# A two-layer adaLN block: a half-size first and last chunk, modulations as weighted sums, grouped low-rank merges, and an opening in written order

## Chip, core and metric

The kernel runs on one core of a Trainium2 chip. The metric is the device time of one execution in microseconds (us); lower is better. All arithmetic is fp32.

## The reference, cut to what matters

Input x is [2048, 512]: 2048 tokens of 512 channels. Two layers follow, each with six modulation rows of 512 from a condition vector c (`wmod` is [512, 3072]):

```python
mod = (silu(c) @ wmod).reshape(1, 6, 1, 512); sa, ca, ga, sb, cb, gb = mod.swapaxes(0, 1)
ga = sign(ga) * max(|ga|, 0.25); gb = sign(gb) * max(|gb|, 0.25)

# layer 0: block-masked linear, then a gated MLP of 1376 hidden units, every weight with a rank-16 update
x = x + ga * (( layernorm(x) * (1 + ca) + sa) @ (weight * blockmask).T + bias)
h = layernorm(x) * (1 + cb) + sb
x = x + gb * lora(silu(lora(h, gate)) * lora(h, up), down)      # lora(x, w) = x @ w.T + (x @ a.T) @ b.T

# layer 1 (its own c and wmod): a Mamba mixer of 1024 channels and 16 states, then top-2 of 8 rank-16 experts
xz = (layernorm(x) * (1 + ca) + sa) @ W_in.T;  u = silu(causal_conv4(xz[:, :1024]))
ts, B, C = rms(u @ W_x.T split 32, 16, 16);    dt = softplus(ts @ W_dt.T + b_dt)
state = state * exp(dt * A) + (dt * u) * B     # per channel and state, a scan over the 2048 tokens
y = sum over states(state * C) + u * D
x = x + ga * ((y * silu(xz[:, 1024:])) @ W_out.T)
h = layernorm(x) * (1 + cb) + sb
x = x + gb * (h @ base_W.T + 2 * sum over the top 2 experts(rw * (h @ A_e) @ B_e))
```

## The kernel before

Tokens are cut into eight chunks of 256 (`TC`, `NC`, `NM` = 2 token tiles of 128). Channels lie on partitions; the eight channel tiles of the scan (`ND`) lie side by side in one free dimension, so that one scan instruction of 128x2064 takes a whole chunk for one state (8 x (256 + 2 padding)).

**Opening.** Everything is scheduled by the framework's planner, engine by engine, from its cost model. `mod_col` makes a modulation column with 16 small matmuls over four loaded weight tiles (L118), `mod_gate` a gate row with four wide matmuls on a spread condition vector (L126 to L142). The attention weight is masked (L199 to L208) and scaled by the gate. `wide_tile` (L231) loads a gate or up tile, makes its low-rank product with four matmuls of 16 rows (L241), adds it on DVE (L245) and stores the merged tile to DRAM scratch; `down_tile` (L249) does this for the down projection after a scaling on POOL. Chunks after the first read the merged tiles back. `first_layer(0)` runs to its end, then layer one's columns are made, then `front(0)`: norm, input projection (L371), convolution (L391), the small projection, `steps` (softplus, L427), `inputs` and the first `decays`.

**Norm.** `norm_t` (L144): stats on DVE, two POOL instructions for the inverse deviation (L151, L152), the subtraction and scaling on DVE (L156), transposes on PE (L164) and modulation on ACT (L167).

**Main loop** (L654 to L702). For each chunk and each of 16 states: hb = dt*u*B (L669) and the scan (L671) on DVE, hc = h*C (L677) on DVE, PE transposes that add hc into four PSUM banks `ys` (L441), and `decays` for the next state on ACT (L458). `da`, `hb` and `hc` have two buffers each. Between the states, two generators are advanced by budgets: `first` (layer 0 of the next chunks) by 3.6 per state, 8.0 for the first eight states of chunk 0; `second` (`beside(c)`: out_proj and experts of the chunk before, gate_proj of this one, `front` of the next) by 4.8, or 2.5. `late_setup` (the second layer's remaining modulations and the scaled W_out, written to scratch) runs beside chunk 0, its loads on ACT's queue. Streamed weights are loaded on SP's queue into twelve `ws` buffers; `rows_bc` broadcasts B and C three states ahead, on SP as well.

**Tail.** After the last state the last chunk's gating, out_proj and experts run alone.

Of the kernel before, what the change touches and what calls it, by code (L numbers as in the profile page):

```python
# [9 lines left out]
FP = mybir.dt.float32  # L10
# [7 lines left out]
P = 128  # L18
L, DM = 2048, 512
TC = 256  # L20
NC, NM, NK = L // TC, TC // P, DM // P
# [5 lines left out]
SEG = TC + 2  # L27
# [10 lines left out]
def mamba_block_kernel(  # L38
# [36 lines left out]
    def halves(t):  # L75
        return t.rearrange("p (a n) -> p a n", a=2)
# [9 lines left out]
    ones = keep.tile([1, P], FP, name="ones")  # L86
# [4 lines left out]
    def load(c):  # L91
        xs[c] = []
        for i in range(c * NM, (c + 1) * NM):
            xt = xpool.tile([P, DM], FP, tag="x", name="x")
            nc.sync.dma_start(out=xt, in_=x_in[i * P : (i + 1) * P, :])
            xs[c].append(xt)

    da = [keep.tile([P, ND, SEG], FP, name=f"da{i}") for i in range(2)]
    hb = [keep.tile([P, ND, SEG], FP, name=f"hb{i}") for i in range(2)]
    hc = [keep.tile([P, ND, TC], FP, name=f"hc{i}") for i in range(2)]  # L100
    dtu = keep.tile([P, ND, TC], FP, name="dtu")
    dt = keep.tile([P, ND, TC], FP, name="dt")
    states = keep.tile([P, NS, ND], FP, name="states")

    def mod_weights(wmod, j, queue):
        wms = []
        for k in range(NK):
            wm = ws()
            queue.dma_start(out=wm, in_=wmod[k * P : (k + 1) * P, j * DM : (j + 1) * DM])
            wms.append(wm)  # L110
        return wms

    def mod_col(name, sc, wmod, j, queue):
        wms = mod_weights(wmod, j, queue)
        ps = bank()
        for f in range(NK):
            for k in range(NK):
                T.matmul(  # L118
                    ps[:, f : f + 1], lhsT=wms[k][:, f * P : (f + 1) * P], rhs=sc[:, k : k + 1],
                    start=k == 0, stop=k == NK - 1,  # L120
                )
        col = keep.tile([P, NK], FP, name=f"mod_{name}{j}")
        V.tensor_scalar(col, ps[:, :NK], 1.0 if j in (1, 4) else 0.0, None, ALU.add)
        return col

    def spread(sc):  # L126
        scb = tmp()
        scb3 = scb.rearrange("p (k m) -> p k m", k=NK)
        V.tensor_copy(scb3, sc.unsqueeze(2).to_broadcast([P, NK, P]))
        return scb3  # L130

    def mod_gate(scb3, wmod, j, queue):
        wms = mod_weights(wmod, j, queue)
        ps = bank()
        for k in range(NK):
            T.matmul(ps, lhsT=scb3[:, k, :], rhs=wms[k], start=k == 0, stop=k == NK - 1)
# [7 lines left out]
    def norm_t(xt, scale, shift, tag):  # L144
        st = small.tile([P, NM, 6], FP, tag="st", name="st")
        mv = small.tile([P, NM, 2], FP, tag="mv", name="mv")
        for m in range(NM):
            V.bn_stats(st[:, m, :], xt[m])
            V.bn_aggr(mv[:, m, :], st[:, m, :])  # L149
        rs = small.tile([P, NM], FP, tag="rs", name="rs")  # L150
        G.tensor_scalar(rs, mv[:, :, 1], LN_EPS, None, ALU.add)  # L151
        G.tensor_tensor(rs, rs, power, ALU.pow)  # L152
        xn = []
        for m in range(NM):
            t = tmp()
            V.tensor_scalar(t, xt[m], mv[:, m, 0:1], rs[:, m : m + 1], ALU.subtract, ALU.mult)  # L156
            xn.append(t)
        h = hpool.tile([P, NK, TC], FP, tag=tag, bufs=2 if tag == "h0" else 1, name="h")
        for k2 in range(NK // 2):
            ps = halves(bank())  # L160
            for i in range(2):
                k = 2 * k2 + i
                for m in range(NM):
# [6 lines left out]
            yield 0.5  # L170
# [6 lines left out]

    load(0)
    S.activation(c0_sb, c0_sb, AF.Silu)
    w_attn = [ws() for k in range(NK)]  # L180
    for k in range(NK):
        nc.scalar.dma_start(out=w_attn[k], in_=w_attn_t[k * P : (k + 1) * P, :])
# [3 lines left out]
    for k in range(NK):  # L186
        mk = wsp.tile([P, DM], I32, tag="w", name="mk")
        nc.scalar.dma_start(out=mk, in_=mask_t[k * P : (k + 1) * P, :])
# [3 lines left out]

    sa, ca = (mod_col("a", c0_sb, wmod0, j, nc.sync) for j in (0, 1))
    scb0 = spread(c0_sb)
    ga = mod_gate(scb0, wmod0, 2, nc.sync)

# [7 lines left out]
    V.tensor_scalar(on, ps[:, :nb], 0.0, None, ALU.is_gt)  # L204
    for k in range(NK):
# [3 lines left out]
    attn_s = dram.tile([NK, P, DM], FP, name="attn_s")  # L209
    for k in range(NK):  # L210
        V.tensor_tensor(w_attn[k], w_attn[k], ga, ALU.mult)
        nc.gpsimd.dma_start(out=attn_s[k], in_=w_attn[k])
    V.tensor_tensor(bias_row, bias_row, ga[0:1, :], ALU.mult)

    sb, cb = (mod_col("a", c0_sb, wmod0, j, nc.scalar) for j in (3, 4))
    gb = mod_gate(scb0, wmod0, 5, nc.scalar)

    ranks = [hc[0].rearrange("p t n -> p (t n)")[:R, i * DM : (i + 1) * DM] for i in range(3)]
    wides = [t.rearrange("p t n -> p (t n)")[:R, :FF] for t in (da[0], da[1], hb[0])]
    for dst, src in zip(ranks + wides, (gate_a, up_a, down_bt, gate_bt, up_bt, down_a)):  # L220
        nc.gpsimd.dma_start(out=dst, in_=src)
    ga_r, ua_r, db_r = ranks
    gb_w, ub_w, da_w = wides
    V.tensor_tensor(db_r, db_r, gb[:R, :], ALU.mult)

    gate_s = dram.tile([len(HT), P, DM], FP, name="gate_s")
    up_s = dram.tile([len(HT), P, DM], FP, name="up_s")
    down_s = dram.tile([len(HT), P, DM], FP, name="down_s")
    wout_s = dram.tile([ND, P, DM], FP, name="wout_s")

    def wide_tile(src, scratch, a_r, b_w, j, first):  # L231
        h0, n = HT[j]
        w = ws()
        w3 = w[:, : NK * n].rearrange("p (k n) -> p k n", k=NK)
        if not first:
            nc.sync.dma_start(out=w[:, : NK * n], in_=scratch[j][:, : NK * n])
            return w3
        nc.sync.dma_start(out=w3, in_=src.rearrange("(k p) n -> p k n", p=P)[:, :, h0 : h0 + n])
        ps = bank()
        for k in range(NK):  # L240
            T.matmul(  # L241
                ps[:, k * n : (k + 1) * n], lhsT=a_r[:, k * P : (k + 1) * P], rhs=b_w[:, h0 : h0 + n],
                start=True, stop=True,
            )
        V.tensor_tensor(w[:, : NK * n], w[:, : NK * n], ps[:, : NK * n], ALU.add)  # L245
        nc.gpsimd.dma_start(out=scratch[j][:, : NK * n], in_=w[:, : NK * n])
        return w3

    def down_tile(j, first):  # L249
        h0, n = HT[j]  # L250
        w = ws()
        if not first:
            nc.sync.dma_start(out=w[:n, :], in_=down_s[j][:n, :])
            return w
        nc.sync.dma_start(out=w[:n, :], in_=down_t[h0 : h0 + n, :])
        G.tensor_tensor(w[:n, :], w[:n, :], gb[:n, :], ALU.mult)
        ps = bank()
        T.matmul(ps[:n, :], lhsT=da_w[:, h0 : h0 + n], rhs=db_r, start=True, stop=True)
        V.tensor_tensor(w[:n, :], w[:n, :], ps[:n, :], ALU.add)
        nc.gpsimd.dma_start(out=down_s[j][:n, :], in_=w[:n, :])  # L260
        return w

    done = set()

    def first_layer(c):
        xt = xs[c]
# [515 lines left out]
```

## Time and profile before

| | |
|---|---|
| three runs | median 1860.17 us (1859.12 to 1862.04) |
| the profiled execution | 1859.38 us, span 1857.6 us |
| first scan starts | 246.9 us |
| 128 scans of 128x2064 | 4.45 us each |
| hb and hc, 128x2048 | 2.28 us each |
| decays on ACT, 128x256, 1024 of them | 0.50 us each |
| busy over the span | PE 84%, DVE 80%, ACT 51%, POOL 12% |

PE is the matmul engine (its weight loads are listed apart, as PEld), DVE the vector engine, ACT the scalar engine, POOL the GpSimd engine, SP the engine that only issues DMAs. Every fp32 matmul appears as two matmul records. Lines are those of the kernel before.

### The profile page before, as it was taken

What the parts mean: (1) busy time and instruction counts of PE and PEld (TensorE: products, weight loads), DVE (VectorE), ACT (ScalarE), POOL (GpSimd) and SP (SyncE); (2) the same over time, 40 slices, a digit from 0 to 9 for tenths busy, and PEclk for the clock granted to TensorE, in tenths of its full rate; (3) what the DMA queues carried; (4) which work ended last, traced back from release to release, by engine and by line L of the source; (5) the groups of instructions that cost most, each with busy time, mean ns of one, the idle gap of its engine ahead of it and who ended that gap; (6) DMA issues with size and microseconds to landing.
All of it is one profiled execution on the core that took longest, in us unless ns stands there. A gap on an engine that the chain in (4) does not pass through costs nothing. (4 is left out here: it accounts for less than half of the span.)

```text
span 1857.6 us, 18733 instructions
## 1 busy us (share of the span) xinstructions
PE 1562.9 (84%) x6568; PEld 1079.8 (58%) x6568; DVE 1483.0 (80%) x1215; ACT 938.9 (51%) x2005; POOL 225.7 (12%) x211
## 2 busy tenths in 40 slices
PE   4899879988698888999799888999899789768646
PEld 4685647756465665576456665576557565544433
DVE  2222387797978989897999789897989799999992
ACT  0110367445654565565565566466556555674521
POOL 0123010013000200031003300160003000300000
PEclk9689779988998989999899999999999999879768
DMA  8544333562343234432343334422333235213100
GB/s 251 154 154 165 116 86 115 166 198 85 91 126 108 86 93 120 129 102 89 91 137 106 94 100 123 116 83 89 116 115 100 80 104 149 67 35 100 28 20 12
DMA packets 157536, 199.73 MB, mean 108 GB/s; under 512 B 14962, under 2 KB 93682, under 8 KB 157443
## 3 DMA queue, kind: packets, MB, share of 16 engines
q1 hardware_dynamic: 141984, 166.57, 31.0%
q10 hardware_dynamic: 10434, 15.81, 2.6%
q0 software_dynamic: 5024, 16.16, 2.4%
q8 instruction: 52, 0.85, 0.2%
q14 instruction: 42, 0.34, 0.1%
HBM read 182.43 MB, written 16.06 MB: 107 GB/s over the span
## 5 line engine op out<-in xcount | busy, mean ns | idle before, releaser
L671 DVE TENSOR_TENSOR_SCAN hb<-da,hb 128x2064 f32<-128x2064 f32 x128 | 568.7, 4449 | 3.5
L458 ACT ACTIVATE da<-dt,neg_a 128x256 f32<-128x256 f32 x1024 | 430.4, 497 | 55.9 <-DVE hb L671 43.1
L298 PE MATMUL ps<-h,ws 128*128 128x256 f32 (+1 forms) x1408 | 352.6, 407 | 19.6 <-ACT z L481 13.0
L441 PE MATMUL y<-ident,hc 128*128 128x128 f32 x2048 | 287.0, 293 | 65.5 <-DVE hc L677 65.3
L298 PEld LDWEIGHTS ps<-h,ws 128*128 128x128 f32 (+1 forms) x1408 | 281.6, 204 | 93.2 <-issue 19.6
L441 PEld LDWEIGHTS y<-ident,hc 128*128 128x128 f32 x2048 | 255.1, 152 | 117.8 <-DVE hc L677 75.4
L677 DVE TENSOR_TENSOR hc<-hb,bcn 128x2048 f32<-128x2048 f32 x128 | 291.4, 2278 | 35.8 <-PE y L441 35.6
L669 DVE TENSOR_TENSOR hb<-dtu,bcn 128x2048 f32<-128x2048 f32 x128 | 290.7, 2281 | 2.7
L673 ACT COPY states<-hb 128x8 f32<-128x8 f32 x112 | 22.8, 203 | 348.0 <-DVE hb L671 340.1
L151 POOL TENSOR_SCALAR rs<-mv 128x2 f32<-128x2 f32 x32 | 41.3, 1292 | 1155.4 <-DVE mv L149 1139.5
L508 PE MATMUL ps<-ws,tmp 128*128 128x512 f32 x256 | 136.3, 671 | 47.3 <-ACT tmp L502 47.1
L317 PE MATMUL ps<-ws,hidden 128*128 128x512 f32 (+1 forms) x352 | 159.0, 601 | 5.7 <-ACT z L481 4.9
L371 PE MATMUL ps<-h,ws 128*128 128x256 f32 x512 | 122.2, 394 | 2.5 <-ACT h L167 2.5
L476 PE MATMUL ps<-ws,h 128*128 128x512 f32 x256 | 117.1, 604 | 1.1 <-ACT hidden L306 0.6
L317 PEld LDWEIGHTS ps<-ws,hidden 128*128 128x128 f32 (+1 forms) x352 | 65.7, 192 | 85.1 <-issue 71.7
L371 PEld LDWEIGHTS ps<-h,ws 128*128 128x128 f32 x512 | 100.3, 199 | 21.3 <-ACT h L167 5.8
L508 PEld LDWEIGHTS ps<-ws,tmp 128*128 128x128 f32 x256 | 51.2, 214 | 101.3 <-ACT tmp L502 53.5
L309 DVE TENSOR_TENSOR hidden<-hidden,tmp 128x512 f32<-128x512 f32 x40 | 27.6, 690 | 85.1 <-ACT tmp L307 85.1
L391 DVE SCALAR_TENSOR_TENSOR tmp<-xp,ch,tmp 128x256 f32<-128x256 f32 x192 | 79.7, 476 | 13.1 <-ACT tmp L386 12.6
L458 ACT ACT_TABLE_LOAD x67 | 86.0, 1283 | 1.0
L164 PE MATMUL ps<-ident,tmp 128*128 128x128 f32 x256 | 48.7, 329 | 41.4 <-DVE tmp L156 38.0
L379 POOL COPY xp<-halo 128x6 f32<-128x6 f32 x28 | 71.0, 2537 | 77.2 <-DVE tmp L391 66.7
(137 smaller groups left out, 1575.0 us busy)
## 6 DMA issues: line engine op xcount, KB each, us to landing
bcn<-bc SPq DMA_DIRECT2D x128, 256.0 KB, 5.1
ws<-gate_s SPq DMA_DIRECT2D x70, 256.0 KB, 2.7
ws<-up_s SPq DMA_DIRECT2D x70, 256.0 KB, 2.7
ws<-down_s SPq DMA_DIRECT2D x70, 256.0 KB, 3.8
ws<-win_x_t_dram SPq DMA_DIRECT2D x64, 256.0 KB, 3.8
ws<-win_z_t_dram SPq DMA_DIRECT2D x64, 256.0 KB, 2.9
ws<-wout_s SPq DMA_DIRECT2D x64, 256.0 KB, 2.6
ws<-wmod_dram ACTq DMA_DIRECT2D x36, 256.0 KB, 3.2
```

The lines of the kernel that those rows point to most:

```text
L298: T.matmul(ps[:n, i, :], lhsT=w3[:, k, :], rhs=h[:, k, :], stop=k == NK - 1, **start_only(4 * i + k),)
L317: T.matmul(acc[m], lhsT=hidden[j // 2][:n, j % 2, m * P : (m + 1) * P], rhs=w[:n, :], start=j == 0, stop=j == len(HT) - 1,)
L371: T.matmul(ps[:, i, :], lhsT=w3[:, k, :], rhs=h[:, k, :], stop=k == NK - 1, **start_only(4 * i + k),)
L379: G.tensor_copy(xp[:, :, : KC - 1], halo[:, 2 * t2 : 2 * t2 + 2, :])
L391: V.scalar_tensor_tensor(acc[:, i, :], xp[:, i, j : j + TC], ch[:, t, C_W + j : C_W + j + 1], acc[:, i, :], ALU.mult, ALU.add,)
L441: T.matmul(ys[m][a][:, i * P : (i + 1) * P], lhsT=src[:, m * P : (m + 1) * P], rhs=ident, start=first and i == 0, stop=last, is_transpose= ...
L458: S.activation(d[:, t, 2:], dt[:, t, :], AF.Exp, scale=neg_a[:, t, n : n + 1])
L476: T.matmul(acc[m], lhsT=h[:, k, m * P : (m + 1) * P], rhs=w, start=k == 0, stop=k == NK - 1)
L508: T.matmul(acc[m], lhsT=g[:, i, m * P : (m + 1) * P], rhs=w, start=t == 0, stop=t == ND - 1)
L669: V.tensor_tensor(h[:, :, 2:], dtu, bcn[:, 0:1, :].to_broadcast([P, ND, TC]), ALU.mult)
L671: V.tensor_tensor_scan(flat_h, flat_d, flat_h, 0.0, ALU.mult, ALU.add)
L677: V.tensor_tensor(hcn, h[:, :, 2:], bcn[:, 1:2, :].to_broadcast([P, ND, TC]), ALU.mult)
```

## The change

The chunks become one of 128 tokens, seven of 256 and one of 128, with the buffers viewed at the chunk's width. A modulation row becomes a weighted sum of four weight tiles (one pass on ACT, three on DVE), summed over partitions by matmuls with ones. The low-rank rows are copied to partitions 0, 32, 64 and 96, and the merges of four tiles are made together with one matmul from each row group into the four banks of `ys`. The norm's subtraction moves to ACT, with two more POOL instructions for its bias. PE and DVE keep the written order until the first decays. `late_setup` moves from chunk 0 to chunk 1, its modulation loads and those of W_out from ACT's queue to SP's; the budgets are given anew.

```diff
-NC, NM, NK = L // TC, TC // P, DM // P
+SIZES = [1, 2, 2, 2, 2, 2, 2, 2, 1]
...
+    def mod_row(sc, wmod, j, wm=None):
...
+        acc = tmp()
+        S.activation(acc, wm[0], AF.Identity, scale=sc[:, 0:1])
+        for k in range(1, NK):
+            V.scalar_tensor_tensor(acc, wm[k], sc[:, k : k + 1], acc, ALU.mult, ALU.add)
+        return acc
     def mod_col(...):
-        for f in range(NK):
-            for k in range(NK):
-                T.matmul(ps[:, f : f + 1], lhsT=wms[k][:, f * P : (f + 1) * P], rhs=sc[:, k : k + 1], ...)
+        acc = mod_row(sc, wmod, j, wm)
+        for f in range(NK):
+            T.matmul(ps[:, f : f + 1], lhsT=acc[:, f * P : (f + 1) * P], rhs=ones[:, 0:1], start=True, stop=True)
     def mod_gate(...):
-        for k in range(NK):
-            T.matmul(ps, lhsT=scb3[:, k, :], rhs=wms[k], start=k == 0, stop=k == NK - 1)
+        acc = mod_row(sc, wmod, j, wm)
+        T.matmul(ps, lhsT=ones, rhs=acc, start=True, stop=True)
...
     def norm_t(xt, scale, shift, tag):
-        G.tensor_scalar(rs, mv[:, :, 1], LN_EPS, None, ALU.add)
-        G.tensor_tensor(rs, rs, power, ALU.pow)
+        G.tensor_scalar(rs[:, 0, :], mv[:, :, 1], LN_EPS, None, ALU.add)
+        G.tensor_tensor(rs[:, 0, :], rs[:, 0, :], power[:, :nm], ALU.pow)
+        G.tensor_tensor(rs[:, 1, :], mv[:, :, 0], rs[:, 0, :], ALU.mult)
+        G.tensor_scalar(rs[:, 1, :], rs[:, 1, :], -1.0, None, ALU.mult)
-            V.tensor_scalar(t, xt[m], mv[:, m, 0:1], rs[:, m : m + 1], ALU.subtract, ALU.mult)
+            S.activation(t, xt[m], AF.Identity, bias=rs[:, 1, m : m + 1], scale=rs[:, 0, m : m + 1])
...
+    def merge_wide(tiles, scratch, a_r, b_w, js):
+        h0, n = HT[js[0]][0], sum(HT[j][1] for j in js)
+        for k in range(NK):
+            r = slice(32 * k, 32 * k + R)
+            T.matmul(y_all[:, k, :n], lhsT=a_r[r, k * P : (k + 1) * P], rhs=b_w[r, h0 : h0 + n], start=True, stop=True)
+        for w3, j in zip(tiles, js):
+            V.tensor_tensor(w3, w3, y_all[:, :, o : o + m], ALU.add)
+            nc.gpsimd.dma_start(out=scratch[j]..., in_=w3)
+    def merge_down(tiles, js):              # the same by groups of four down tiles
...
+        ahead = {                           # in first_layer(0): before the product of hidden tiles j0, j0 + 1
+            0: lambda: merge_next(0, 1),
+            2: lambda: merge_next(1, 1),
+            4: lambda: merge_next(0, 2),
+            6: lambda: (merge_next(1, 2), second_gate()),
+            8: lambda: merge_down_next(0),
+        }
...
+                if j == 6:                  # in first_layer(0), down projection
+                    mods1.extend(mod_col("b", c1_sb, wmod1, q, wms[q]) for q in (0, 1))
...
+    order = ExitStack()
+    order.enter_context(tc.manual_schedule(engines={mybir.EngineType.PE, mybir.EngineType.DVE}))
+    for q in (0, 3, 1, 4, 2, 5):            # rank rows, to four row groups
+        for r0 in range(0, P, 32):
+            (nc.scalar if q in (2, 5) else nc.gpsimd).dma_start(out=ranked[q][0][r0 : r0 + R, :], in_=ranked[q][1])
+    wms = [four(t) for t in (dt_b, dtu_b, hc_b[1])]
+    sa, ca = (mod_col("a", c0_sb, wmod0, j, wms[j]) for j in (0, 1))
+    opening = first_layer(0); next(opening); next(opening)
+    merge_next(0, 0); merge_next(1, 0)
...
     def beside(c):
+        if c == 1:
+            yield from late_setup()
         if c > 0:
             yield from out_proj(c - 1)
         yield from gate_proj(c)
-        if c == 0:
-            yield from late_setup()
...
     steps(0); inputs(0); bcs = [rows_bc(0, n) for n in range(3)]
-    decays(0)
+    decays(0, 0)
+    order.close()
...
-            budget = 4.8 if c > 0 or n > 7 else 2.5
-            spare += budget
+            if c == 0:
+                one, two = (7.0, 1.0) if n < 9 else (0.0, 8.0)
+            elif c == 1:
+                one, two = (7.0, 2.5) if n < 9 else (3.6, 5.5)
+            else:
+                one, two = (4.1, 4.8)
+            spare += two
...
-            left = run_first(left + (3.6 if c > 0 or n > 7 else 8.0) + (0.0 if finished else max(spare, 0.0)))
+            left = run_first(left + one + (0.0 if finished else max(spare, 0.0)))
```

## The prediction

> **What bounds the kernel now.** I read the page's first part, then the busy time by stretch, cut at every sixteenth scan (the scans of one chunk of tokens), then the timeline of the opening and of the tail, and last the rows of single lines.
>
> ```profile
> span 1857.6 us, 18733 instructions
> ...
> PE 1562.9 (84%) x6568; PEld 1079.8 (58%) x6568; DVE 1483.0 (80%) x1215; ACT 938.9 (51%) x2005; POOL 225.7 (12%) x211
> ```
>
> No engine is full over the whole span. By stretch (columns: us; busy time and count of PE, PEld, DVE, ACT, POOL; granted clock; DMA share; GB/s):
>
> ```profile
> 0.00:46.90 46.90, 23.34 (x90) 19.45 (x91) 10.02 (x24) 3.89 (x6) 4.45 (x16) 0.97 0.82 251
> 46.90:90.20 43.30, 37.13 (x125) 25.64 (x126) 12.05 (x24) 5.75 (x10) 4.87 (x9) 0.70 0.50 152
> 90.20:157.30 67.10, 67.10 (x321) 57.16 (x320) 16.07 (x24) 6.30 (x11) 23.54 (x31) 0.83 0.48 154
> 157.30:189.00 31.70, 30.86 (x67) 11.60 (x67) 8.59 (x13) 0.37 (x1) 7.32 (x13) 1.00 0.54 178
> 189.00:246.90 57.90, 50.01 (x195) 38.48 (x194) 25.53 (x48) 26.30 (x51) 3.21 (x12) 0.71 0.34 105
> 246.90:468.30 221.40, 194.33 (x843) 137.94 (x841) 187.80 (x147) 122.50 (x246) 30.90 (x26) 0.89 0.44 133
> 468.30:674.60 206.30, 175.06 (x751) 119.37 (x752) 178.07 (x140) 113.47 (x247) 18.30 (x18) 0.93 0.37 104
> ...
> 883.30:1081.10 197.80, 173.46 (x752) 117.52 (x752) 177.82 (x140) 118.14 (x256) 29.72 (x18) 0.94 0.37 107
> ...
> 1664.10:1806.40 142.30, 92.03 (x374) 62.96 (x374) 140.48 (x77) 64.71 (x158) 4.03 (x4) 0.73 0.19 48
> 1806.40:1857.60 51.20, 34.84 (x110) 20.09 (x110) 13.38 (x36) 5.30 (x12) 2.08 (x4) 0.86 0.03 11
> ```
>
> Three kinds of time are seen. An opening of 246.9 us before the first scan, DVE 72 us busy in it and PE the bound (67.1 of 67.1 us in the third row). Full chunks of about 200 us, PE and DVE both near 88%. The last chunk, DVE alone (140.5 of 142.3), and a tail of 51.2 us, a serial chain on the last 256 tokens. In the opening the rows that carry the time are:
>
> ```profile
> 68.59 8.72 PE L280 MATMUL ps<-ws,h 128*128 128x512 f32 x16
> ...
> 104.86 9.38 PE L298 MATMUL ps<-h,ws 128*128 128x256 f32 x32
> ...
> 117.93 7.17 PE L298 MATMUL ps<-h,ws 128*128 128x256 f32 x32
> ...
> 125.04 3.83 PE L241 MATMUL ps<-da,hc 16*128 16x128 f32 x32
> ```
> ```profile
> 189.04 11.61 PE L118 MATMUL ps<-c_sb,ws 128*128 128x1 f32 x64
> ...
> 203.95 2.00 PE L164 MATMUL ps<-ident,tmp 128*128 128x128 f32 x8 [3.29 <-DVE tmp L156]
> ```
>
> Attention begins only at 68.6; each pair of hidden tiles costs a merge (L241) and a product (L298) one behind the other; at 189 the second layer's modulations hold PE before the norm that front(0) waits for. Every fp32 matmul shows as two passes.
>
> **Opening (246.9 us now).** Six terms.
> (a) To the attention's start, 68.6. Three modulation columns (3.1 MB), eight gate and up tiles (2.1), attention weight and mask (2.1), x and the four copies of the rank rows (1.7) must land first: 9.0 MB, at the first row's 251 GB/s 36 us. Then the gate's weighted sum (one ACT pass 0.6, three DVE passes of 0.69), one ones matmul and the chain that took 42.1 to 49.5 before: some 12. Sum 48.
> (b) Attention and second norm, 68.6 to 90.2 (21.6 us): half the L280 passes (8 of 0.54 = 4.4), two weighted sums ahead of the residual on DVE (5), norm 6 with its new POOL pair. 14, though part of the sums waits beside PE.
> (c) Gate and up, 67.1 us. 176 product passes of 128 columns: no such row, so between 0.13 (PE's 128x128 transposes, 8 in 1.04 us) and 0.25 (the same at the lower granted clock of the opening, 8 in 2.00); L298 itself takes 0.22 to 0.29 for 256 columns. I take 0.19, 33 us. Merges: 48 passes of 512 columns in place of 176 of 128; at 0.46 to 0.54 each (L317, L280) 22 to 26 us if they follow one another, as now, and a quarter, 6, if the four row groups run at once. No row shows it; I take 12, nearer to the lower end as the four write four banks. Their DVE adds (22 of 0.69) lie beside PE. Sum 45, with gaps 49.
> (d) Down, 31.7 us: 22 L317 passes in place of 44 (10), merges in groups (22 passes of 0.46 = 10, or 3), the wait of 1 us per pair for the DVE add mostly gone. 15.
> (e) The PE block at 189 (to 204, 15 us) becomes six DVE passes and eight small matmuls inside (d): 2.
> (f) Norm, front, ssm, steps, first decays: 204 to 246.9 (43 us). It is a chain; L371 and the convolution halve (15 to 8, 11 to 7), the fixed ends stay: 32.
> Sum 160, a gain of 87. Bounds: 135 (row groups overlap, warm clock, all of (e) hidden) and 200 (no overlap, cold passes throughout, and SP waiting for up tiles of group 2, whose buffers are freed only after group 0's products).
>
> The Trainium skill, TensorEngine Tiling (Array Packing), Theoretical Speedup, gives up to 4x for a contraction of at most 32 and, under Key Properties, says that changing the tiling mode drains the array; by the first the merges of (c) would be the 6 us, by the second something is given back at each of nine switches, which no row here prices. TensorE: Matmul & The Clock Gate, Part 1, says that the array falls to half rate after an idle window; it speaks against a thinner stream of half-width products, and by it (c) would be priced at the cold end, 44 us for the products, 11 more than I take.
>
> **Main loop.** A half-size step: hb and hc 1.22 each (from 0.69 for 512 and 2.28 for 2048), the scan 2.3 (4.45 by 1040/2064, a little fixed): 4.75 against 9.01 for a full one. So 32 half steps cost 8 us more than 16 full ones.
>
> Chunk 0 (128 tokens) must still carry layer one and front of chunk 1 (256 tokens). PE: 176 L298 passes of 0.22 (39), 44 L317 and 20 attention passes of 0.46 (29), 64 L371 of 0.24 (15), the small ones and transposes 10, gate projection 7, y transposes 136 of 0.14 (19): 119 us. DVE: 16 of 4.75 and 26 of other work, 102. PE is the bound; at the 0.85 that it reaches in full chunks 140, with the boundary (30 to 42 us from a chunk's last scan to the next chunk's first, now under less scan cover) 145. So 221.4 becomes 145, for half of the tokens.
>
> Chunk 1 takes late_setup from chunk 0: 8 weight scalings, 5 for w_base, twelve weighted-sum passes, some 20 us of DVE, against 8 saved since out_proj(0) and experts(0) are half, and 24 loads that pass from ACT's queue to SP's, ahead of the streamed weights, which may hide there. With the norms' 4 off, DVE has 8 more than the second chunk's 178.1 before, PE some 12 fewer than its 175.1; I take that chunk's 206.3 less 1: 205.
>
> Chunks 2 to 6 are full. The norm's subtraction leaves DVE (8 per chunk of 0.54 = 4.3 us) for ACT (8 of about 0.75, from L167's 0.56 for 256 and ACT's 0.2 per further 256; ACT is 58% busy there). Each of the four norms per chunk gets two more POOL instructions:
>
> ```profile
> L151 POOL TENSOR_SCALAR rs<-mv x32: 217/222/4392, 12.7 to 1832.5; 128x2 f32<-128x2 f32 x32
> L152 POOL TENSOR_TENSOR rs<-rs,power x32: 708/721/2797, 13.1 to 1832.8; 128x2 f32<-128x2 f32 x32
> L156 DVE TENSOR_SCALAR tmp<-x,mv,rs x64: 442/541/547, 64.7 to 1834.0; 128x512 f32<-128x512 f32 x64
> ```
>
> The median of L151 is 0.22 us, the worst 4.39, as long as a scan; mean 1.29. So the pair costs 0.4 to 8.8 us of latency per norm, some 2.6 by the mean. Against it the subtraction no longer queues behind a scan on DVE (PE waited 38.0 us in 17 times for L156). I let these cancel on PE and keep most of the DVE gain, as both engines bind: the mean of the five full chunks before, 202.4, hence five of 197. Ends: 190 (DVE sets it, 0.92 busy) and 206.
>
> Chunk 7 is like the seventh stretch before (183.6, layer one finished early), with half a front: 178. Chunk 8: 16 of 4.75 and 13 for gating and experts of chunk 7 on DVE, 89; PE's 56 us lie beside.
>
> **Tail, 51.2 us.** Halved: out_proj's 32 passes of 0.46 (7.4 saved), y and the last hc (2.8), gating (1.3), one tile's residual, stats and norm products (4); the base product no longer ends after the router chain (2.5). 33.
>
> **Sum.** 160 + 145 + 205 + 985 + 178 + 89 + 33 = 1795 of span, and 1.8 around it (1859.38 less 1857.6) makes 1797. That execution is 0.8 us under the median of 1860.17, so no correction is due.
>
> **Rivals.** (1) The full chunks follow DVE: the five take 190 each (35 less), chunk 1 loses 7 as well, the opening nears 145 (15 less). 1740. For it: both engines idle only 20 us per chunk and DVE's load falls. Against: PE is as full and loses nothing there. (2) The opening gains little: 200, since SP's loads wait for buffers, or the row groups do not run side by side (the change then does not do what it says). 40 more: 1837. Against: PE's own work of the opening falls from 208 us to about 110. (3) Slower: the longer norm chain. PE runs in order, so a late norm stops all transposes and products behind it, y among them, and then hc and the scans. If both new POOL instructions wait out a scan, 32 norms in the loop gain up to 8.8 us each; from 2 us per norm net the gain of 62 is spent, at 2.7 the time is 1883. For it: L151's 4.39. Against: both follow directly upon each other, so that one wait serves both, and ACT starts freely.
>
> **Chances.** The forecast 0.46, rival 1 0.20, rival 2 0.20, rival 3 0.14. About 0.2% (3.7 us) is what a measurement of this kernel can tell. Rival 2's upper edge and rival 3's lower edge meet near 1860, 0.02. Faster 0.84, same 0.02, slower 0.14. The range goes from 1730 (rival 1 with the opening at its bound of 135) to 1855, above rival 2 with the full chunks 4 us longer each, and leaves out rival 3 alone.
>
> **What would show it.** First scan at 160 (135 to 200); the second chunk's first scan 145 later; L156's work under ACT, DVE busy 30 us less in the loop; a merge of eight passes in under 2 us where row groups overlap; the last scan 33 before the end. I am wrong if the full chunks lengthen past 206 with PE waiting for ACT's norm output, or if the first scan comes after 210.

## The result and the profile after

The changed kernel takes **1914.60 us** (median of 4 runs, 1905.56 to 1917.62) against 1861.11 us of the kernel before, measured beside it: a ratio of **1.0281 [1.0245, 1.0317]**, 53 us slower. The forecast was 1797 and its range ended at 1855. The larger part of the miss, 62 of 118 us, is the third rival, the longer norm chain, which had been given 0.14; the rest is spread over the opening and the chunks.

First the totals, from the first part of the page of the kernel after.

```profile
span 1913.2 us, 19261 instructions
...
PE 1500.2 (78%) x6498; PEld 1037.0 (54%) x6498; DVE 1498.0 (78%) x1291; ACT 1065.2 (56%) x2334; POOL 309.1 (16%) x310
```

PE has 63 us less to do than before and DVE 15 more, yet the span is 56 us longer. So the loss is waiting, not work. The busy time by stretch, cut at every sixteenth scan as before, shows where (columns: us; busy time and count of PE, PEld, DVE, ACT, POOL; granted clock; DMA share; GB/s). The rows are the opening, chunks 0 to 8 and the tail. The last cut, at 1877.5, lies 2.2 us behind the end of the last scan (1875.3, a scan of half width takes 2.29), so by the scans chunk 8 is 85.6 and the tail 37.8.

```profile
0.00:184.30 184.30, 102.40 (x457) 68.95 (x458) 78.97 (x141) 40.50 (x89) 53.13 (x96) 0.87 0.72 222
184.30:343.60 159.30, 133.82 (x541) 93.16 (x539) 104.66 (x107) 111.81 (x251) 15.71 (x22) 0.87 0.38 110
343.60:584.90 241.30, 190.09 (x813) 133.76 (x813) 196.19 (x171) 127.07 (x266) 43.59 (x41) 0.88 0.42 130
584.90:788.60 203.70, 181.36 (x783) 125.11 (x784) 174.81 (x131) 122.53 (x262) 32.12 (x26) 0.93 0.39 108
788.60:998.80 210.20, 183.72 (x788) 127.47 (x786) 176.82 (x135) 128.32 (x268) 44.07 (x26) 0.93 0.37 105
998.80:1216.10 217.30, 181.49 (x770) 126.49 (x768) 175.71 (x134) 124.64 (x264) 36.18 (x26) 0.89 0.35 97
1216.10:1428.30 212.20, 174.27 (x751) 120.89 (x750) 175.13 (x133) 124.49 (x264) 35.87 (x26) 0.91 0.37 96
1428.30:1630.90 202.60, 170.68 (x816) 117.28 (x814) 173.15 (x134) 131.00 (x279) 27.50 (x26) 0.92 0.45 124
1630.90:1789.80 158.90, 103.75 (x499) 75.11 (x499) 155.66 (x111) 102.65 (x243) 11.09 (x10) 0.82 0.27 67
1789.80:1877.50 87.70, 58.04 (x235) 37.75 (x236) 80.32 (x80) 47.87 (x146) 7.99 (x6) 0.81 0.19 60
1877.50:1913.20 35.70, 20.61 (x60) 11.06 (x58) 6.57 (x27) 4.36 (x12) 1.86 (x5) 0.79 0.02 8
```

The first scan comes 62.6 us earlier than before (184.3 against 246.9), and the tail is some 13 shorter (51.2 to 37.8). But the full chunks 2 to 6 take 209.2 us each instead of 202.4, and chunk 1 takes 241.3. In the rows of chunks 2 to 6 PE is busy 171 to 184 us and DVE 173 to 177: they now stand idle for 22 to 38 and 29 to 42 us in each.

Who makes PE wait is in the list of waits (us in all, times, longest us). Before, then after:

```profile
PE ps L164 <- DVE tmp L156: 38.0, 17, 5.4
DVE hc L677 <- PE y L441: 35.6, 20, 4.3
```
```profile
ACT tmp L168 <- POOL rs L164: 177.6, 19, 30.3
...
PE ps L176 <- ACT tmp L168: 118.1, 28, 15.5
...
DVE hc L778 <- PE y_all L532: 69.8, 39, 5.2
```

PE's wait for the normalised tile has trebled, 38.0 to 118.1 us. It now ends on ACT, which itself waited 177.6 us for L164, the last of the four POOL instructions. This is the sign of being wrong that the prediction named: full chunks past 206 us with PE waiting for ACT's norm output. And DVE waits twice as long as before for PE's y (69.8 against 35.6 us). One norm of chunk 1 shows the whole chain, in the timeline after (start and length in us, and the idle time before):

```profile
373.78 2.17 POOL L161 TENSOR_SCALAR rs<-mv 128x2 f32<-128x2 f32 x1 [3.40 <-DVE mv L159]
375.78 4.45 DVE L772 TENSOR_TENSOR_SCAN hb<-da,hb 128x2064 f32<-128x2064 f32 x1
376.03 4.72 POOL L162 TENSOR_TENSOR rs<-rs,power 128x2 f32<-128x2 f32 x1
380.83 0.20 POOL L163 TENSOR_TENSOR rs<-mv,rs 128x2 f32<-128x2 f32 x1
381.11 0.23 POOL L164 TENSOR_SCALAR rs<-rs 128x2 f32<-128x2 f32 x1
381.38 1.52 ACT L168 ACTIVATE tmp<-x,rs 128x512 f32<-128x512 f32 x2 [17.76 <-POOL rs L164]
...
382.25 2.25 PE L176 MATMUL ps<-ident,tmp 128*128 128x128 f32 x8 [15.53 <-ACT tmp L168]
```

L161 takes 2.17 us beside hb on DVE and L162 4.72 beside the scan; L163 takes 0.20 where DVE stands idle. PE stood for 15.5 us and none of the products behind the transposes ran in that time. In this norm the two that were slowed are the two that the kernel before had as well, and the added pair took 0.43. In another, in chunk 3, the added pair is slowed too, by the scan and by hb:

```profile
937.07 3.70 POOL L163 TENSOR_TENSOR rs<-mv,rs 128x2 f32<-128x2 f32 x1
...
940.86 2.19 POOL L164 TENSOR_SCALAR rs<-rs 128x2 f32<-128x2 f32 x1
```

Over the whole span, minimum, median and maximum in ns:

```profile
L162 POOL TENSOR_TENSOR rs<-rs,power x36: 571/720/4921, 31.6 to 1891.8; 128x2 f32<-128x2 f32 x28, 128x1 f32<-128x1 f32 x8
...
L163 POOL TENSOR_TENSOR rs<-mv,rs x36: 190/196/4400, 32.2 to 1892.5; 128x2 f32<-128x2 f32 x28, 128x1 f32<-128x1 f32 x8
L164 POOL TENSOR_SCALAR rs<-rs x36: 223/233/2307, 32.5 to 1892.7; 128x2 f32<-128x2 f32 x28, 128x1 f32<-128x1 f32 x8
...
L168 ACT ACTIVATE tmp<-x,rs x64: 797/805/818, 37.0 to 1893.0; 128x512 f32<-128x512 f32 x64
```

So the two added instructions usually take 0.2 us, but they too can meet a scan, up to 4.40 us. In the trace one of the two takes over 1 us in 13 of the 36 norms, in 9 of these after L161 or L162 had already taken over 1 us; both do in one norm alone. Summed over the 36 norms, the four take 48.4, 51.4, 39.1 and 15.2 us. ACT's subtraction takes 0.81 us in every case.

The opening by terms: to attention, attention and second norm, gate and up, down, and the chain to the first scan.

```profile
0.00:75.60 75.60, 17.57 (x58) 10.67 (x59) 27.96 (x50) 9.37 (x16) 14.69 (x36) 1.00 1.05 311
75.60:89.30 13.70, 9.35 (x22) 3.63 (x21) 1.56 (x3) 3.15 (x6) 3.05 (x5) 0.81 0.33 120
89.30:129.50 40.20, 34.98 (x223) 28.36 (x219) 24.36 (x34) 6.69 (x17) 22.83 (x29) 0.81 0.52 174
129.50:152.00 22.50, 16.79 (x48) 8.38 (x44) 9.73 (x17) 0.53 (x1) 8.48 (x11) 0.77 0.71 237
152.00:184.30 32.30, 23.71 (x117) 17.91 (x118) 15.35 (x39) 20.76 (x51) 4.08 (x16) 0.74 0.35 106
```

Four of the five terms are within 10 us of the forecast; the first is 28 us late. PE's rows in the second and third, from the timeline, correspond to those of L280, L298 and L241 before:

```profile
75.60 6.26 PE L282 MATMUL ps<-hb,h 128*128 128x512 f32 x8
...
87.26 2.09 PE L204 MATMUL y_all<-da,hc 16*128 16x512 f32 x8
89.28 3.78 PE L317 MATMUL ps<-h,ws 128*128 128x128 f32 x16
...
95.49 1.14 PE L204 MATMUL y_all<-da,hc 16*128 16x512 f32 x8
96.56 2.05 PE L317 MATMUL ps<-h,ws 128*128 128x128 f32 x16
```

Eight merge passes take 2.09 us, later 1.14; a product pass of 128 columns 0.24, later 0.13. The timeline of ACT in the first term tells what it stood at (ACTq is ACT issuing a DMA; the row of four holds the issues and the time between them):

```profile
4.63 16.00 ACTq L371 DMA_DIRECT2D hb<-down_a_dram  x4
20.74 0.72 ACT L126 ACTIVATE tmp<-dt,c_sb 128x512 f32<-128x512 f32 x1 [16.34 <-DMA ws<-gate_t_dram]
...
47.54 0.33 ACTq L389 DMA_DIRECT2D tmp<-block_in_dram  x1
47.92 0.72 ACT L126 ACTIVATE tmp<-hc,c_sb 128x512 f32<-128x512 f32 x1 [10.12 <-DMA dt<-wmod_dram]
```

ACT computes nothing from 4.6 to 20.7 us, the stretch in which it issues four loads. The issues themselves take 0.3 to 0.7 us each; the third starts at 7.93 and the fourth at 20.32. The gate's weighted sum begins only at 47.9, just behind the issue of the block matrix. The forecast had attention starting at 48.

### The profile page after: what moved, and what is told of

It reads as the page before. It is cut to its first block, busy times and chain, and to the rows that moved or that the text cites. A ratio compares the mean times of both kernels' runs of the same rounds, so it can differ in the third digit from the quotient of the medians.

```text
span 1913.2 us, 19261 instructions
## 1 busy us (share of the span) xinstructions
PE 1500.2 (78%) x6498; PEld 1037.0 (54%) x6498; DVE 1498.0 (78%) x1291; ACT 1065.2 (56%) x2334; POOL 309.1 (16%) x310
## 5 line engine op out<-in xcount | busy, mean ns | idle before, releaser
L772 DVE TENSOR_TENSOR_SCAN hb<-da,hb 128x2064 f32<-128x2064 f32 (+1 forms) x144 | 571.4, 3974 | 9.6 <-ACT da L552 5.4
L552 ACT ACTIVATE da<-dt,neg_a 128x256 f32<-128x256 f32 (+1 forms) x1152 | 459.1, 474 | 24.9 <-DVE hb L772 23.9
L532 PE MATMUL y_all<-ident,hc 128*128 128x128 f32 x2048 | 288.7, 293 | 94.7 <-DVE hc L778 94.6
L778 DVE TENSOR_TENSOR hc<-hb,bcn 128x2048 f32<-128x2048 f32 (+1 forms) x144 | 293.6, 2044 | 70.4 <-PE y_all L532 69.8
L317 PE MATMUL ps<-h,ws 128*128 128x256 f32 (+3 forms) x1496 | 332.0, 378 | 7.0 <-ACT z L576 3.4
L532 PEld LDWEIGHTS y_all<-ident,hc 128*128 128x128 f32 x2048 | 255.6, 152 | 149.8 <-DVE hc L778 105.8
L770 DVE TENSOR_TENSOR hb<-dtu,bcn 128x2048 f32<-128x2048 f32 (+1 forms) x144 | 293.1, 2046 | 4.4 <-ACT states L774 1.3
L161 POOL TENSOR_SCALAR rs<-mv 128x2 f32<-128x2 f32 (+1 forms) x36 | 48.4, 1345 | 971.7 <-DVE mv L159 898.4
L168 ACT ACTIVATE tmp<-x,rs 128x512 f32<-128x512 f32 x64 | 49.4, 807 | 181.7 <-POOL rs L164 177.6
L176 PE MATMUL ps<-ident,tmp 128*128 128x128 f32 x256 | 55.0, 354 | 118.2 <-ACT tmp L168 118.1
L481 DVE SCALAR_TENSOR_TENSOR tmp<-xp,ch,tmp 128x256 f32<-128x256 f32 (+1 forms) x216 | 84.3, 449 | 63.3 <-ACT tmp L476 62.3
L461 PE MATMUL ps<-h,ws 128*128 128x256 f32 (+1 forms) x576 | 123.9, 373 | 6.4 <-ACT h L179 6.2
```

What stands on the lines that cost most here:

```text
L176: T.transpose(ps[:, i, m * P : (m + 1) * P], xn[m][:, k * P : (k + 1) * P], ident)
L317: T.matmul(ps[:n, i, :], lhsT=w3[:, k, :], rhs=h[:, k, :], stop=k == NK - 1, **start_only(4 * i + k),)
L461: T.matmul(ps[:, i, :], lhsT=w3[:, k, :], rhs=h[:, k, :], stop=k == NK - 1, **start_only(4 * i + k),)
L481: V.scalar_tensor_tensor(acc[:, i, :], xp[:, i, j : j + w_c], ch[:, t, C_W + j : C_W + j + 1], acc[:, i, :], ALU.mult, ALU.add,)
L532: T.matmul(ys[m][a][:, i * P : (i + 1) * P], lhsT=src[:, m * P : (m + 1) * P], rhs=ident, start=first and i == 0, stop=last, is_transpose= ...
L552: S.activation(d[:, t, PAD:], dt[:, t, :], AF.Exp, scale=neg_a[:, t, n : n + 1])
```

## The experiments

Ratios are to the kernel before, measured beside each run, with their 95% intervals. Spans and stages are of the profiled execution, which can lie some us off the median: with the norm on DVE it took 1853.31 against a median of 1846.80. The theory: the norm's longer chain costs what the main loop lost. Two rivals: the chunk sizes cost it; or the pacing budgets of the main loop do.

**Norm back on DVE.** After, with the old norm: two POOL instructions, the subtraction on DVE.

```diff
-        G.tensor_tensor(rs[:, 1, :], mv[:, :, 0], rs[:, 0, :], ALU.mult)
-        G.tensor_scalar(rs[:, 1, :], rs[:, 1, :], -1.0, None, ALU.mult)
-            S.activation(t, xt[m], AF.Identity, bias=rs[:, 1, m : m + 1], scale=rs[:, 0, m : m + 1])
+            V.tensor_scalar(t, xt[m], mv[:, m, 0:1], rs[:, m : m + 1], ALU.subtract, ALU.mult)
```

> The changed kernel with the norm's subtraction back on DVE and without the two added POOL instructions; all else as changed. Theory N (the longer norm chain makes PE wait in order: 118 us of PE waiting for the norm's ACT output, 38 for DVE's before): the full chunks go from 209 back to about 201, chunk 1 from 241 to about 225, in all 50 to 70 less, 1850 to 1865 us. Rival B (the new budgets crowd the chunks) and rival L (the layout in nine chunks costs a boundary): no gain, since DVE takes back 4 us per chunk: 1912 to 1935.

Measured 1846.80, ratio 0.9942 [0.9924, 0.9961]: faster than before, and 68 us faster than after by the medians, 62.0 by the spans (1913.2 to 1851.2). The waits of this run:

```profile
PE ps L174 <- DVE tmp L166: 34.4, 15, 10.8
```

PE's wait falls from 118.1 to 34.4 us, which is 84 us, more than the whole gain. DVE is busy 28 us longer (1525.8 against 1498.0) and the kernel is still faster.

**The norm's change alone, on the kernel before.** The reverse edit: the POOL pair and ACT's subtraction, nothing else.

> The kernel before with the norm's change alone (subtraction on ACT, two POOL instructions more). Theory N: 32 norms, some 2 us each on PE's path, less 4 us per chunk of DVE: 1880 to 1920 us against 1861. Rivals B and L: the norm's move is harmless or helps, 1835 to 1862.

Measured 1896.39, ratio 1.0214 [1.0184, 1.0244], some 39 us slower than before. PE's wait rises as well:

```profile
PE ps L166 <- ACT tmp L158: 97.8, 23, 11.7
```

Shown from both sides: this one part of the change loses 39 us by itself, in 32 norms, and 62 within the whole, in 36.

**The pacing budgets.** After, with less layer-one work per step from chunk 2 on: `one, two = (4.1, 4.8)` becomes `(3.6, 4.8)`.

> The changed kernel with layer one's budget from chunk 2 on back from 4.1 to 3.6 per state. Rival B: the five full chunks lose some 7 us each, 1875 to 1890 us. Theory N: within 10 us of the changed kernel's 1914.

Measured 1927.92, ratio 1.0380 [1.0347, 1.0413], 13 us slower than after and outside both expectations. The rival of the budgets falls for this direction; a larger budget was not tried.

**Eight equal chunks.** After, with `SIZES = [2] * 8`.

> The changed kernel with eight chunks of 256 as before; opening, norm and late_setup as changed. Rival L (nine chunks lose a boundary of 20 to 30 us and gain little): opening about 210, chunk 0 about 210, tail 51, in all 1870 to 1895 us. Theory N with the layout worth what was forecast (opening, chunk 0, last chunk and tail together some 20 us better than eight equal chunks): 1925 to 1945.

Measured 1918.58, ratio 1.0330 [1.0310, 1.0350]. First scan 228.4, tail 56.3. That is between the two expectations. The 44 us that the short first chunk saves before the first scan and the 18 in the tail are nearly all spent again from the first scan to the last (1691 us in nine chunks, 1630 in eight); the layout is worth 4 us by the medians and 9 by the ratios, whose intervals overlap a little. The rival of the sizes falls: the sizes do not cost the loss, but they do not bring the gain either.

**The bias by one DVE operation.** Which link of the chain costs? The subtraction stays on ACT; the two added POOL instructions become one on DVE.

```diff
-        G.tensor_tensor(rs[:, 1, :], mv[:, :, 0], rs[:, 0, :], ALU.mult)
-        G.tensor_scalar(rs[:, 1, :], rs[:, 1, :], -1.0, None, ALU.mult)
+        V.scalar_tensor_tensor(rs[:, 1, :], mv[:, :, 0], -1.0, rs[:, 0, :], ALU.mult, ALU.mult)
```

> The changed kernel with the norm's subtraction left on ACT, but its bias made by one small DVE instruction instead of the two added POOL instructions. If the POOL pair is what lengthens the chain, most of the 68 us come back: 1850 to 1865. If the step over to ACT is (its queue of decays and table loads, and two engine hops more), little does: 1895 to 1915. Both parts: between.

Measured 1869.88, ratio 1.0057 [1.0042, 1.0072]. By the spans (1913.2, 1867.9, 1851.2) 45 of the 62 us come back. The other 17 (23 by the medians) are the step over ACT, with the bias as an operation of its own on DVE ahead of it. PE's wait is 10 us above that with the norm on DVE:

```profile
PE ps L175 <- ACT tmp L167: 44.9, 19, 11.1
```

But the edit does two things. It takes the pair out of the chain, and it gives DVE an instruction that waits for L162. The row of L162 (ns), and what DVE waited for before the bias (us, times):

```profile
L162 POOL TENSOR_TENSOR rs<-rs,power x36: 567/715/854, 33.1 to 1847.7; 128x2 f32<-128x2 f32 x28, 128x1 f32<-128x1 f32 x8
...
  POOL rs L162: 31.9, 34
```

In 34 of the 36 norms DVE stands and waits for L162, and L162 never takes more than 0.85 us; after, where DVE has no part in the chain behind the mean and streams on, it took up to 4.92. L161 and L162 together take 58.8 us here against 99.8 after, so they are 41 us shorter; the pair that is gone had taken 54.3. The 45 us are therefore what the chain gained in both ways, and no run parts them.

**The POOL pair off the chain.** As the last, with the pair kept but writing a tile that nobody reads.

```diff
+        off = small.tile([P, nm], FP, tag="off", name="off")
+        G.tensor_tensor(off, mv[:, :, 0], rs[:, 0, :], ALU.mult)
+        G.tensor_scalar(off, off, -1.0, None, ALU.mult)
```

> The changed kernel with the norm's bias made on DVE (1869.9), and the two POOL instructions kept, writing a tile that nobody reads. If they cost as links of the norm's chain: 1865 to 1878. If they cost as load on POOL, which shares its turn with DVE and is waited for by the convolution's copies and the next norm: 1895 to 1915.

Measured 1868.39, ratio 1.0047 [1.0032, 1.0062]; without the pair it was 1.0057 [1.0042, 1.0072]. The pair costs nothing as load: not on POOL, and not through what it may do to DVE beside it. The 45 us are a matter of the chain between the mean and the transposes: of its two added links, and of the first two, which DVE no longer waits for.

The next experiments ask about the rest, the opening and chunk 1, with the norm on DVE.

**late_setup beside chunk 0.** Chunk 1 took 230.8 us with the norm on DVE, against a forecast of 205.

```diff
-        if c == 1:
-            yield from late_setup()
...
         yield from gate_proj(c)
+        if c == 0:
+            yield from late_setup()
```

> The kernel with the norm on DVE (1846.8), and late_setup back beside chunk 0, after gate_proj. Theory S (late_setup's weighted sums stand in the way of chunk 1, where DVE is full, while chunk 0 leaves DVE idle for 46 of 153 us): chunk 1 from 231 to about 208, chunk 0 up by 5 to 10, 1828 to 1838. Rival (PE binds chunk 0, so its work only changes place, and chunk 1's length has another cause): 1843 to 1855.

Measured 1842.26, ratio 0.9908 [0.9893, 0.9923]. Chunk 1 falls from 230.8 to 216.4 us, chunk 0 rises from 153.3 to 159.6. So of the 26 us above the forecast some 14 are the place of late_setup. The whole gains 4.5 us by the medians, less than theory S expected.

**Chunk 1 with the budgets of the later chunks.** The last, without the branch that gives chunk 1 budgets of its own.

> The kernel with the norm on DVE and late_setup beside chunk 0, and chunk 1 with the budgets of the later chunks (4.1 and 4.8) instead of 7.0/2.5 and 3.6/5.5. Chunk 1 takes 216 us where the later ones take 200. If its budgets are the cause: 200 to 206 in chunk 1, 1828 to 1835 in all. If the lead that they give layer one is needed later: the gain returns in chunks 2 to 6, 1840 to 1850.

Measured 1848.66, ratio 0.9932 [0.9908, 0.9956], no gain. In the profiled execution, the fastest of the four (1841.41), chunk 1 is 213.6 us, 2.8 shorter, and chunk 2 is 204.6 instead of 199.1. The remaining 12 us of chunk 1 stand beside a chunk 7 of 162.6 where 178 was forecast; but chunk 7 stays at 162.4 here, so that layer one's lead is only moved between the two is not shown, and the cause stays open.

**One row group.** Do the four row groups run at once? With the norm on DVE, all merges from row group 0.

```diff
-            r = slice(32 * k, 32 * k + R)
+            r = slice(0, R)
...
-            r = slice(32 * i, 32 * i + R)
+            r = slice(0, R)
```

> The kernel with the norm on DVE, and all merges of a group made from row group 0, so that its four matmuls can't run side by side. If the row groups run at once (8 passes took 1.14 us at the higher clock), a group takes 3.5 to 4 us instead: nine groups 2.5 us more each, some of it behind loads: 10 to 25 us slower in the opening, 1857 to 1870. If they don't: no change, 1843 to 1850.

Measured 1868.74, ratio 1.0054 [1.0035, 1.0073]; the first scan moves from 183.7 to 203.8. Lots of eight merge passes at L202, first from row group 0 alone, then in four groups (norm on DVE):

```profile
92.36 7.19 PE L202 MATMUL y_all<-da,hc 16*128 16x512 f32 x8
...
105.37 3.70 PE L202 MATMUL y_all<-da,hc 16*128 16x512 f32 x8
```
```profile
88.91 2.09 PE L202 MATMUL y_all<-da,hc 16*128 16x512 f32 x8
96.22 1.14 PE L202 MATMUL y_all<-da,hc 16*128 16x512 f32 x8
```

7.19 to 2.09 and 3.70 to 1.14: factors of 3.4 and 3.2. In the lots from one group the granted clock was 0.50 and 1.00, as it was in those of the kernel after, which take the same 2.09 and 1.14. The groups do run side by side, and this part of the change does what it says.

**The written order of the opening.** With the norm on DVE, the merges of group 0 and the layer's scale and shift sums (sb, cb) written after the attention.

```diff
-    merge_next(0, 0)
-    merge_next(1, 0)
...
+    for _ in range(5):
+        next(opening)
     sb, cb = (mod_col("a", c0_sb, wmod0, j, wms[j - 3]) for j in (3, 4))
+    merge_next(0, 0)
+    merge_next(1, 0)
```

> The kernel with the norm on DVE, and in the opening the first group's merges (2 MB of loads) and the sums for sb and cb written after the attention's matmuls instead of before. Theory O (the opening loses 24 us on the forecast because the gate's column lands at 47.5 behind 8 MB that others wait for, and because PE stands at the sb and cb sums for 8 us): attention starts near 52 instead of 75, first scan near 165, 1825 to 1835. Rival (the bytes are the bound whatever their order, and the first products wait for the group's tiles instead): first scan 180 to 185, 1842 to 1850.

A miss: 1853.79, ratio 0.9967 [0.9957, 0.9978], the first scan at 190.8 instead of 183.7. Attention did start earlier, at 68.2 instead of 77.8, but not near 52, as the gate's sum still began only at 48.97. And the residual now stood on DVE behind the merges' adds, at 89.7 instead of 84.5.

**Only the two sums later.** Norm on DVE, late_setup beside chunk 0, and only the line with `next(opening)` put ahead of sb and cb.

> The kernel with the norm on DVE and late_setup beside chunk 0, and only the sums for sb and cb written after the attention's matmuls, the merges left where they are. If PE's written order holds the attention back by these sums, it starts at 66 instead of 75 and the first scan comes 5 to 9 us sooner: 1833 to 1838. If the residual then waits for the same sums on DVE: 1840 to 1845.

Measured 1839.25, ratio 0.9887 [0.9868, 0.9905], whose interval overlaps that of late_setup beside chunk 0. Attention starts at 66.7 instead of 75.8, as expected, but the first scan only at 179.3 instead of 181.6: most of the 9 us are lost again behind it.

**ACT issues no loads.** Norm on DVE, late_setup beside chunk 0, and the loads of the opening and of late_setup that ACT issued (all but x) on SP: `nc.scalar.dma_start` becomes `nc.sync.dma_start`.

> The kernel with the norm on DVE and late_setup beside chunk 0 (1842.3), and every load that ACT issued in the opening and in late_setup issued by SP instead, but x. Theory A (ACT's instruction stream stands at its own DMA issues: 16 us at the rank rows before the first weighted sum at 20.7, and 10 to 15 us at the block matrix before the gate's sum at 47.9): first sum near 13, attention starts near 62 instead of 75, first scan 165 to 172, 1826 to 1834. Rival (the sums wait for their bytes, at 277 GB/s, whoever issues them): first scan 180 to 186, 1838 to 1850.

Measured 1839.22, ratio 0.9890 [0.9875, 0.9904]; first scan 177.5. That is 4 us, not the 10 and more that were expected. The first weighted sum begins at 17.19, not near 13, and only 3.6 us earlier than after: most of the 16 us behind the four issues did not come back. The gate's sum begins 10.7 us earlier than after, at 37.22, but ACT then stands at the activation of c1, a column that arrives late and that no step of layer one needs yet:

```profile
37.22 0.72 ACT L126 ACTIVATE tmp<-hc,c_sb 128x512 f32<-128x512 f32 x1 [5.67 <-DMA hc<-wmod_dram]
...
47.76 0.20 ACT L418 ACTIVATE c_sb<-c_sb 128x4 f32<-128x4 f32 x1 [9.81 <-DMA c_sb<-c_dram]
```

**ACT clear to the attention.** The last two together, with c1 activated right behind c0, and the block that makes neg_a written behind the opening.

```diff
     S.activation(c0_sb, c0_sb, AF.Silu)
+    c1_sb = keep.tile([P, NK], FP, name="c1_sb")
+    nc.sync.dma_start(out=c1_sb, in_=c1)
+    S.activation(c1_sb, c1_sb, AF.Silu)
...
+    for _ in range(5):
+        next(opening)
     sb, cb = (mod_col("a", c0_sb, wmod0, j, wms[j - 3]) for j in (3, 4))
...
+    for _ in opening:
+        pass
     neg_a = keep.tile([P, ND, NS], FP, name="neg_a")
```

> The kernel with the norm on DVE, late_setup beside chunk 0 and ACT's loads on SP (1839.2), and in addition: the sums for sb and cb after the attention's matmuls, the second condition vector's load and silu first of all, neg_a after the opening. Theory A (ACT's in-order stream holds the gate's column; it stood at 47.8 for the condition vector while the gate's matmul had ended at 44.5): attention starts near 56, first scan 163 to 169, 1824 to 1832. Rival (the opening is bound by its bytes or by DVE's written order): first scan 175 to 180, 1835 to 1842.

Measured 1834.37, ratio 0.9862 [0.9843, 0.9882]; first scan 172.8, attention at 60.59. Still above what was expected, in part for the same kind of reason as the last time. The gate's matmul ends at 43.81, but the exponential for neg_a stands on ACT ahead of the gate's next step (L147) and waits for its own load, some 3 us:

```profile
46.47 0.31 ACT L432 ACTIVATE neg_a<-ch 128x128 f32<-128x128 f32 x1 [8.47 <-DMA ch<-chan_dram]
46.69 0.58 ACT L147 ACTIVATE tmp<-ps 128x512 f32<-128x512 f32 x1
```

**Eight equal chunks again, with the norm on DVE.** Is the layout worth more once the norm is out of the way? `SIZES = [2] * 8`, first with late_setup beside chunk 0.

> The kernel with the norm on DVE and late_setup beside chunk 0, in eight chunks of 256. What the layout alone is worth. By the eight-chunk run with the changed norm (1918.6 against 1914.6): 1842 to 1852. By the sum of the forecast (opening 25 us longer, chunk 0 about 55 for its further 128 tokens, tail 18, against a ninth chunk's 85 and 16 of chunk 7): no more than 10 us either way.

Measured 1840.50, ratio 0.9898 [0.9882, 0.9915]; the nine chunks gave 0.9908 [0.9893, 0.9923]. No difference. With the cleared opening as well:

> f1 in eight chunks of 256. Eight and nine were equal to 2 us with the opening as changed (1840.5 and 1842.3), so 1822 to 1834, within 6 of f1. If the shorter first chunk profits more from a clear opening: 8 to 15 above f1.

Measured **1830.91, ratio 0.9840 [0.9824, 0.9855]**, against 0.9862 [0.9843, 0.9882] for the nine chunks with the same opening. The intervals overlap. This is the lowest time measured; it keeps the sums, the row groups and the opening in written order, and leaves out the chunk sizes and the norm on ACT. First scan 218.1, tail 56.6.

## Why the prediction was wrong, point by point

The forecast span was 1795, the measured one 1913: 118 us. With the norm on DVE it is 1851, so the norm is 62 of them; the opening is 24 of the other 56, chunk 0 8, chunk 1 26 and chunks 2 to 6 15, and chunks 7 and 8 and the tail give 17 back.

**The step that failed: "I let these cancel on PE and keep most of the DVE gain".** The prices were about right: the subtraction takes 0.81 us on ACT (forecast 0.75), and the POOL pair 1.5 us per norm by the mean (54.3 in 36), below the 2.6 set for it. What failed was the netting. The forecast set these 2.6 us per norm, 83 in 32 norms, against the queue on DVE that it would spare, and called it even. Its own line held at most 38.0 us for that, 1.2 per norm, and in 16 of the 32 norms DVE had stood waiting for L152, with no queue to spare:

```profile
  POOL rs L152: 14.0, 16
```

It measured 62 us in 36 norms, 1.7 net per norm, of which 1.25 come back when the bias is made on DVE. The argument against the rival, that one wait serves both instructions, held for the pair by itself, since both were slow in one norm of 36. It left out that the pair meets a streaming DVE anew behind L161 and L162, and that these two grow as well once DVE no longer waits for them (L152 took 0.98 us by the mean before, and 1.36 with the norm's change alone). The DVE gain, 28 us of work, did not come: DVE's wait for y doubled, most likely because PE waited for the norm. The other 17 us, the step over ACT, fit the lengths of the links: 0.16 us for each of 36 biases, and 0.81 against 0.54 for each of 64 tiles, together 23 us as an estimate. A queue for the bias on DVE does not show, as in 34 of 36 norms it starts within 0.04 us of the end of L162; no run isolates the step.

The Trainium skill, GPSIMD Engine Reference, 8. Key points, says that this engine shares its SBUF interfaces with VectorE and contends with VectorE's instructions of two SBUF inputs. The rows here agree: L162 took 0.72 us by the median and 4.72 beside a scan, L163 0.20 and 4.40. The run with the pair off the chain shows that this cost time only where somebody waited for it.

**Opening: 160 forecast, 184.3 measured (bounds 135 to 200).** Term (a) failed, 75.6 instead of 48. It counted 9.0 MB at 251 GB/s. The DMA engines were full until attention (share 1.05) and moved 311 GB/s for 75.6 us, 23.5 MB: the loads of later stages went in between (that of w_base, of late_setup, was issued at 32.99). With attention at 60.6 they were as full (1.05), so what is loaded, and in which order, still counts there. It also gave no price to the issues on ACT's own queue, though ACT makes the weighted sums on which attention waits. Taking late_setup, ACT's issues, the two sums and c1 out of the way made 183.7 into 172.8 and brought attention to 60.6; the other 13 us to the forecast were not found. Term (b) was right, 13.7 for 14. Term (c) was 40.2 for 49: the six lots of merges took 9.5 us together, two of them before attention, nearer to the 6 of row groups at once than to the 22 to 26 in series, and the products 0.13 to 0.24 us for the 0.19 taken. Term (d) with (e) was 22.5 for 17; PE waits 5 us in it (2.5 and 2.6) for the second layer's weighted sums on DVE, which the forecast put at 2 in all. Term (f) was right, 32.3 for 32.

The Trainium skill, TensorEngine Tiling (Array Packing), Theoretical Speedup, gives up to 4x here; the merges show 3.2 and 3.4. The drain at a change of mode, which the page names under Key Properties, was not measured by itself.

**Chunks.** Chunk 0 was 159.3 for 145, of which the norm made 6. Chunk 1 was 241.3 for 205: the norm 10.5, late_setup 14, the rest open. The forecast priced late_setup at 20 us of DVE against 8 saved, and then gave the chunk 1 us less than the old one, on the ground that PE had 12 fewer; PE was in fact busy 190 to 194 us in it, not 163. Chunks 2 to 6 were 1046 for 985; with the norm on DVE 1000, which is 200 each, close to the 202.4 of before. So the norm is 46 of the 61 us, and the other 15 answer to the DVE gain on which the 197 of the forecast rested. Chunk 7 was 158.9 for 178, chunk 8 85.6 for 89.

**Tail: 37.8 for 33**, 5 us late. **The layout.** The forecast summed nine chunks and never set them against eight with the same other parts. In both such comparisons with the norm on DVE no gain of it could be measured: what the short chunks save at the ends (43 and 45 us before the first scan, 19 in the tail) their neighbours pay. That they pay because they prepare a full chunk beside half the scans is how the stages look; no run took it apart.

## What to carry to other kernels

When a step is moved off a full engine, count the links of its dependency chain before the microseconds it frees, and set their price against what the list of waits says the old queue cost: 38.0 us here, while the longer chain cost 62. A median of 0.20 us with a maximum of 4.40 is a price per link, as each link can meet a scan anew. Ask also what the relieved engine does next: before, DVE had stood still for the POOL instructions in half of the norms, and once it streamed on beside them they grew. And what an engine issues or waits for ahead of the first product belongs in the sum: with the loads off ACT's queue the gate's sum began 10.7 us earlier, though the first scan came only 4 us sooner.

## What the runs showed of the hardware

POOL operations on [128x2] took 0.19 to 4.9 us according to what DVE did beside them, and four of them in a chain met this independently. The same L162 took at most 0.85 us where DVE waited for it (34 of 36 norms) and up to 4.92 where it did not. The four loads on ACT's queue show as one row of 16.0 us (L371), with 0.3 to 0.7 us for each issue; ACT computed nothing in it. Eight fp32 merge passes of 512 columns took 1.14 us in four row groups and 3.70 in one, both at a granted clock of 1.00.
